# Slots of an expert kernel taken one block earlier: one at a part's second block, a slot inside the prologue, longer DMA runs and new order lists

## The chip, the cores and the metric

One core of a Trainium2 chip. The metric is the device time of one execution in microseconds (us), the median of several. Five engines work side by side: TensorE (PE, with its weight loads PEld), VectorE (DVE), ScalarE (ACT), GpSimd (POOL) and SyncE (SP, which here only issues DMAs).

## What is computed

Two layers, each a graph attention and a mixture of experts, on x of 128 graphs × 64 nodes × 256, that is N = 8192 tokens. Cut to what matters:

```python
def layer(x, adj, l):
    h = layernorm(x) @ W                       # 256 -> 256
    e = (h @ a1)[:, :, None] + (h @ a2)[:, None, :]    # 64 x 64 of a graph
    if l == 1: e = where(e > 0, e, 0.2 * e)
    x = x + elu(softmax(where(adj > 0, e, -9e15)) @ h)
    t = layernorm(x)
    # router: 8 experts, the best two of each token, softmax of the two
    # layer 0: x = x + t + sum over 2 of c * (gelu(t @ w1[e] + b1[e]) @ w2[e] + b2[e])   (256 -> 256 -> 256)
    # layer 1: x = x +     sum over 2 of c * (relu(t @ w1[e] + b1[e]) @ w2[e] + b2[e])   (256 -> 512 -> 256)
```

All in float32. Each layer has 8192 × 2 = 16384 pairs of token and expert.

## The kernel before

**Blocks.** A layer is 16 blocks of 512 tokens (4 tiles of 128). `attend` does the attention of a block, `route` the router. In `attend` a mask is made from adj on POOL (`cap_g`, L341), then statistics on DVE (their power −0.5 on POOL, L290), the normalisation on ACT (L299), transposes on PE (`pt_g`, L310), `pw_g` (L355), `pe_g` (L381), the exponentials on ACT, the scaling L399/L400 on DVE, the transposes `pp_g` (L404), `pT_bd` (L407 on DVE, L409 on ACT), `po_g` (L415), and the sum with x on DVE (L430 to L438). In `route` come statistics again, `tn_r` (L299, ACT), transposes `pt_r`, the router's product `plT_r` (L492), the transpose of the scores on DVE (`lg_r`, L503), the best two, and the counts of tokens by expert (`pn_r`, L553/L554).

**Lists.** Each expert has a list in HBM. For each tile t of a block, a cast of the positions to integers on DVE (`ix_r`, L582) is followed by two indirect DMAs issued by POOL (L587) which write the 128 rows of `tn_r` to the lists of their first and second expert. A row is 256 values and the token's number, expert and (layer 1) weights: 258 or 260 values, 1032 or 1040 B.

**Slots.** A slot is 256 rows of one expert. `plan` (L656 to L698, 20 small DVE instructions) works out on the chip which lists have 256 rows to give. With it `Slots.take` adds SB = 4 slots at each block from the third of a part on (b ≥ LAG = 2). Layer 0 has two parts (blocks 0 to 8 and 9 to 15), layer 1 one. At a part's end SR = 8 more are taken, and 7 that hold the rests of the lists, each 128 rows of one list, two lists to a slot. That makes 40 + 32 + 68 slots. A slot passes through:
- F: `fetch` reads its rows (`xg`, L780, issued by SP), W: its weights (`wc`, L834, L840, L845, SP; 4 buffers)
- x: transposes `px_s` (L900, PE) and their copy `xT` (L905, DVE)
- h: `ph_s` (L998, PE) with gelu or relu (L1008, ACT)
- y: `py_s` (L1034, PE) and `ys` (L1049, DVE; 4 buffers)
- p: layer 0, an indirect write to `res` (L1070, POOL); layer 1, after w (ACT, L1103), an indirect accumulating write into the output (L1080, POOL), each slot's behind the landing of the last one's.

Layer 1's blocks read `mid` (x with the attention and t) and the two rows of `res` of each token.

**Order.** The instructions of SP, PE, DVE and ACT stand in the order in which the program emits them. POOL's indirect DMAs are ordered by `pooled`. The emission is written out by hand: `PROLOGUE` until block 3's attention is done (aN and rN advance attention and routing of block N by a stage), then for each t from 3 to 31 one of two lists `STEPS` (layer 0, layer 1), in which a1 is attention of block t+1, a2 of t+2, r0, r1, r-1 routing, and x, h, y, p, w, W, F act on the oldest slot that has come so far; a mark ? or ! makes an entry hold only when more than four slots wait, or not. Then `ENDING[0]` and, until all slots are done, `ENDING[1]` in turns. In the prologue C0 and C1 make constants by an iota on POOL and a cast on DVE (`counted`), and F0 does the first fetch and the weights of four slots (`slots.ahead(4)`); no x, h, y or p stands in it.

In L598 the condition of taking is

```python
        if b - (CUT if b >= CUT and l == 0 else 0) >= LAG:
            slots.take(l, b, SB, plan(l, f"p{l}_{b}", SB))
```

and the layouts of `mid`, `res` and of a fetch are

```python
    mid_t = mid.rearrange("(b t p) d -> b p t d", t=TT, p=P)
    res_t = [r.rearrange("(b t p k) d -> b p t (k d)", t=TT, p=P, k=2) for r in res]
                out=xg[:, r, 0 : ROW[l]],
                in_=lists[l][bass.ds(u * rows, n), :].rearrange("(t p) d -> p t d", p=P),
```

so that a partition reads 1 KB rows of `mid`, 2 KB of `res` and two single rows of a list.

Of the kernel before, what the change touches and what calls it, by code (L numbers as in the profile page):

```python
# [16 lines left out]
P = 128  # L17
# [4 lines left out]
TT = 4  # L22
# [12 lines left out]
    "h2 h0 h1 a1 a1 p w h0 p p x0 a1 r-1 p h2 h3? r0 w a1 x1 R2 a1 a1 h1 a1 a1 L r-1 r0 "  # L35
    "r0 r0 x2 a1 h3 x0? x1? a1 r0 y0 r0 p a1 w a1 a1 a2~ r0 r-1 x2? p y1 R2 r-1 r-1 p r0 "
    "h2? a1 x1! p y2 a1 W W A2 r0 h0? p? a2~ r-1 h1? a1 R1 a2 y0 a1 w? y1 r0 h3 p F p R1 "
    "x0? x0 a1 y2 W W x1? r0 x2? x0! p? x1 a1 p a2 a2 x2! R1 a1 w? a1 h2 p a1 w h0 w h1 p "
    "p? y0? y1? x0 p p p a1 y2? p? p? h0 r1 y0 x2 p y1 p? h3 h2 a2 p R1 p x1 x2 r0 r1 p p "
    "r0 h3 F W h1 y2 w W W W E1 x0 p y0 p p a2 y1 x1 y2 Z w r1 r0 r0 r0 r1 W x2 W w W ",  # L40
    "a1 a1 a1 w L r-1 h0 r0 a1 h1 h2 p x0 r0 r0 a1 w x1 r-1 a1 h3 x2 r0 x0? p x0! x1? a1 "
    "R2 r0 a2~ x2? h0 p p R2 a1 a1 h1 a1 h3 r-1 r0 p r-1 h2 r0 p r-1 a1 a2~ a1 a1 r0 y0 "
    "r0 r-1 p a1 p w y1 y2 W W h0? h1? r0 x1! h2? h3? y0 p p? a1 a1 p? y1 a1 w? p p x2 y2 "
    "x0 x1 W W p A2 p a1 x2? a1 a1 x0? a1 W R1 w x2! h0 a2 a2 F h1 x1? p? y0? y1? a2 h2 "
    "a1 y2? W h3 p? x2 w w? x0 p h0 a2 p h1 h2 R1 x1 R1 w h3 p? p y0 r0 w p y1 a1 r1 r0 "
    "y2 W W r0 r1 y0 p p? p r1 p F x0 x1 a2 r0 r0 Z p p w p y1 y2 W E1 p x2 W R1 r0 r1 W ",
]
PROLOGUE = (
    "a0 a1 a0 a2 a0 a0 a0 a1 a1 a2 a0 a0 a2 G0 a1 a0 a0 a0 a1 a1 C0 a2 a0 a1 a0 C1 a0 a0 "
    "a0 a2 a0 a1 a2 a1 B0 a1 a0 a1 a1 B1 a2 a0 a1 a0 a1 a0 a0 a1 a2 a1 a0 a2 a1 a2 a0 a0 "  # L50
    "a2 a0 a3 a0 a0 L5 a1 a0 a3 a1 a1 a2 a2 a0 a0 r0 a2 a2 L4 a2 a1 r0 a1 a2 a1 r0 a1 a1 "
    "a2 r0 a2 r0 r0 a3 a3 a1 r0 a2 a2 a1 a2 a1 a1 a3 a4 P0 a2 r0 a2 a1 r0 r0 r0 r1 a2 r1 "
    "a3 a2 a2 a2 a4 a4 a3 r0 a3 r1 a2 a3 r1 a2 r1 a3 a4 a3 G1 a3 r2 r2 r1 r1 a3 r0 r0 a3 "
    "r2 r1 r0 r0 r1 a3 a3 r0 r2 r1 a3 r2 a3 r2 r0 r1 r2 r0 r0 r2 r0 a4 r0 r0 r2 a3 r1 a3 "
    "r0 r2 r1 r2 a3 r1 a3 a4 r0 r1 a3 r0 r2 r0 a3 r1 r1 r1 r1 r1 r2 r1 r2 a4 r1 r2 r1 r1 "
    "a3 a3 a3 a3 r2 r1 a3 r1 r2 r1 a3 r3 r2 r2 r2 r2 r2 r3 r2 r2 r2 r2 r2 F0 r3 r2 r3 "
)
ENDING = [
    "p h1 x1 x0 p p r p x2 w w h0 W h2 h3 ",
    "h3 w x1 r2 q y0 h0 h1 p y1 y2 W p W p p q x2 h2 x0 p W w p F r w ",  # L60
# [4 lines left out]
def adj_ffn_kernel(  # L65
# [44 lines left out]
    SR = SB * LAG  # L110
# [28 lines left out]
    mid_t = mid.rearrange("(b t p) d -> b p t d", t=TT, p=P)  # L139
    res_t = [r.rearrange("(b t p k) d -> b p t (k d)", t=TT, p=P, k=2) for r in res]  # L140
    sums_t = [mid_t, out_t]

    def part(b):

        return int(b >= CUT)

# [325 lines left out]
    def route(l, b, blk):  # L472
# [125 lines left out]
        if b - (CUT if b >= CUT and l == 0 else 0) >= LAG:  # L598
            slots.take(l, b, SB, plan(l, f"p{l}_{b}", SB))
# [169 lines left out]
    def fetch(sl, name):  # L769

        l, rows = sl["l"], P if sl["rest"] else SL
        xg = slot.tile([P, ST, ROW[1]], F32, tag="xg", name=f"xg_{name}", bufs=8)
        for s, r in sl["of"]:
# [7 lines left out]
                out=xg[:, r, 0 : ROW[l]],  # L781
                in_=lists[l][bass.ds(u * rows, n), :].rearrange("(t p) d -> p t d", p=P),
# [4 lines left out]
    class Slots:  # L787
# [105 lines left out]
        def x(self, k):  # L893
# [32 lines left out]
            if rest:  # L926
# [4 lines left out]
                for _, r in sl["of"]:  # L931
                    n = (r.stop - r.start) * P
                    for t in range(r.start, r.stop):
                        nc.vector.tensor_scalar(
                            le[:, t, 0:n], places[:, 0:n], free[:, t : t + 1], None, ALU.is_ge
                        )
# [397 lines left out]
```

## Time and profile before

| what | us |
|---|---|
| median of 8 runs | 1361.18 |
| lowest, highest | 1354.06, 1367.93 |
| the profiled execution | 1353.56 |
| its span | 1351.8 |
| PE, DVE, POOL, ACT busy | 1154.8, 898.8, 713.0, 653.6 |
| mean granted clock of PE | 0.939 of full |

The profile is of one execution, taken by the hardware. A row of a timeline has the start in us from the span's start, the duration in us (of the whole group, if several instructions are put together), engine, line, operation, the tiles out<-in, the count, and in brackets how long the engine had been idle before and what ended that. A row of waits has the engine and what it was about to do, what it waited for, and the total in us, the number of times and the longest. "remote" there is a wait whose end no semaphore event of the program explains; "issue" is time in which the engine waited for nothing that the profile shows. A row of windows has a stretch, its length, each engine's busy time in it (with the instructions that began in it), the clock granted to PE, the mean busy share of 16 DMA engines, and GB/s.

Full-clock prices of PE, from rows after 725 us: four transposes of 128×128 take 0.44 us, eight passes of 128×256 take 1.73 us. A slot of layer 0 is then 3.9 us (4 px, 8 ph, 8 py) and one of layer 1 7.4 us (4, 16, 16). In layer 0 a block takes about 35 us (`pn_r` of blocks 7, 8, 9: 242.6, 277.2, 312.2), in layer 1 38.4 us from block 6 on.

### The profile page before, as it was taken

The numbers are of one execution on the slowest core, as the hardware profiler recorded it, in microseconds if no ns is written. First come the engines' busy times: TensorE is split into PE (matmuls) and PEld (weight loads), VectorE is DVE, ScalarE is ACT, GpSimd is POOL, SyncE is SP. The second block draws the span as 40 slices with busy tenths as digits, with TensorE's granted clock in tenths as the row PEclk, the third lists the DMA queues.
The fourth block names the chain that finished last, engine by engine and source line by source line (L and its number), as shares of the span: only waits on it lengthen the run. The fifth ranks groups of instructions, "written<-read, shape, count | busy, mean of one in ns | idle before, by whom it ended". The sixth has DMA issues, their size and how long they took to land. (4 is left out here: it accounts for less than half of the span.)

```text
span 1351.8 us, 22479 instructions
## 1 busy us (share of the span) xinstructions
PE 1154.8 (85%) x6176; PEld 974.2 (72%) x6176; DVE 898.8 (66%) x3605; ACT 653.6 (48%) x1548; POOL 713.0 (53%) x698
## 2 busy tenths in 40 slices
PE   6658787877888888778789999999999999999990
PEld 5436665756776766667668888888788888889880
DVE  4767775867667778787677777777687766433330
ACT  5636554645555655446554445455454543333330
POOL 3273555553554655556554465655666656533333
PEclk9868888988898998989899999999999999999995
DMA  7637666666776687798789788888978778999843
GB/s 193 180 121 219 221 195 206 199 211 212 245 220 215 216 291 252 226 302 270 240 267 272 226 219 247 242 246 251 272 211 237 194 208 228 265 275 257 230 94 35
DMA packets 263854, 301.17 MB, mean 223 GB/s; under 512 B 39463, under 2 KB 225070, under 8 KB 263728
## 3 DMA queue, kind: packets, MB, share of 16 engines
q1 hardware_dynamic: 208288, 214.50, 51.8%
q0 software_dynamic: 38544, 68.46, 20.3%
q10 hardware_dynamic: 16896, 16.78, 3.6%
q8 instruction: 49, 0.80, 0.3%
q14 instruction: 77, 0.63, 0.1%
HBM read 202.80 MB, written 98.69 MB: 223 GB/s over the span
## 5 line engine op out<-in xcount | busy, mean ns | idle before, releaser
L998 PE MATMUL ph_s<-xT_s,wc_s 128*128 128x256 f32 (+1 forms) x1760 | 403.6, 378 | 23.4 <-DVE xT_s L905 15.2
L1034 PE MATMUL py_s<-wc_s,hT_s 128*128 128x256 f32 x1648 | 392.2, 387 | 8.7 <-ACT hT_s L1008 6.2
L998 PEld LDWEIGHTS ph_s<-xT_s,wc_s 128*128 128x128 f32 x1760 | 321.6, 197 | 69.9 <-DVE xT_s L905 17.9
L1034 PEld LDWEIGHTS py_s<-wc_s,hT_s 128*128 128x128 f32 x1648 | 310.4, 193 | 56.8 <-ACT hT_s L1008 10.2
L1080 POOL DMA_INDIRECT out_dram<-ys_s,to_s x135 | 213.4, 1581 | 231.1 <-DMA out_dram<-ys_s,to_s 104.4
L587 POOL DMA_INDIRECT lists<-tn_r,ix_r x256 | 248.9, 972 | 144.7 <-issue 83.9
L1070 POOL DMA_INDIRECT res<-ys_s,to_s x142 | 142.7, 1005 | 108.7 <-DVE ys_s L1049 63.3
L1008 ACT ACTIVATE hT_s<-ph_s,b_s 128x256 f32<-128x256 f32 (+1 forms) x284 | 114.0, 459 | 106.1 <-PE ph_s L998 48.7
L355 PE MATMUL pw_g<-gw,xt_g 128*128 128x258 f32 x512 | 127.6, 397 | 9.0 <-ACT wh_g L366 6.0
L1049 DVE TENSOR_TENSOR ys_s<-py_s,tb 128x512 f32<-128x512 f32 (+1 forms) x71 | 47.2, 665 | 128.7 <-PE py_s L1034 74.2
L905 DVE COPY xT_s<-px_s 128x512 f32<-128x512 f32 (+1 forms) x140 | 95.1, 679 | 47.0 <-PE px_s L900 25.8
L1103 ACT ACTIVATE ys_s<-ys_s,cf_s 128x256 f32<-128x256 f32 x135 | 61.5, 500 | 127.4 <-DVE ys_s L1049 116.7
L355 PEld LDWEIGHTS pw_g<-gw,xt_g 128*128 128x128 f32 x512 | 95.5, 196 | 27.8 <-ACT wh_g L366 6.7
L1008 ACT ACTIVATE hT_s<-ph_s,wc_s 128x256 f32<-128x256 f32 (+1 forms) x156 | 61.0, 451 | 63.8 <-issue 37.4
L366 ACT COPY wh_g<-pw_g 128x258 f32<-128x258 f32 x128 | 47.8, 377 | 86.5 <-PE pw_g L355 63.7
L299 ACT ACTIVATE xn_g<-xs,nb_g,rs_g 128x256 f32<-128x256 f32 x128 | 66.3, 589 | 46.9 <-DVE nb_g L293 34.8
L900 PE MATMUL px_s<-ident,xg_s 128*128 128x128 f32 x554 | 85.8, 278 | 0.0
L299 ACT ACTIVATE tn_r<-xb_g,nb_r,rs_r 128x256 f32<-128x256 f32 x128 | 66.2, 588 | 33.2 <-DVE nb_r L293 12.9
L290 POOL TENSOR_TENSOR rs_r<-ve_r,nhalf 128x4 f32<-128x4 f32 x32 | 33.7, 1052 | 88.6 <-DVE c_r L535 42.5
L415 PE MATMUL po_g<-wh_g,pT_bd 128*128 128x256 f32 x256 | 68.9, 415 | 12.9 <-ACT pT_bd L409 8.6
L404 PE MATMUL pp_g<-ident,ee_g 128*64 128x128 f32 x128 | 22.7, 308 | 65.5 <-DVE ee_g L400 60.6
L900 PEld LDWEIGHTS px_s<-ident,xg_s 128*128 128x128 f32 x554 | 70.7, 146 | 10.9 <-DVE ys_s L1049 0.3
(503 smaller groups left out, 1613.5 us busy)
## 6 DMA issues: line engine op xcount, KB each, us to landing
wc_s<-in_w_dram SPq DMA_DIRECT2D x142, 512.0 KB
wc_s<-in_w_dram SPq DMA_DIRECT2D x156, 256.0 KB
xg_s<-lists SPq DMA_DIRECT2D x64, 260.0 KB
xg_s<-lists SPq DMA_DIRECT2D x64, 258.0 KB
yb<-res SPq DMA_DIRECT2D x16, 1024.0 KB
wc_s<-bcat SPq DMA_DIRECT2D x78, 129.0 KB
xs<-in_x_dram SPq DMA_DIRECT2D x16, 512.0 KB
mid<-xb_g ACTq DMA_DIRECT2D x16, 512.0 KB
```

The costliest lines, as they stand in the source:

```text
L299: nc.scalar.activation(outs(t), xb[:, t, :], AF.Identity, bias=nb[:, t : t + 1], scale=rs[:, t : t + 1])
L355: nc.tensor.matmul(pw, lhsT=xt[:, k, t * P : (t + 1) * P], rhs=gw[l][:, k, :], start=(k == 0), stop=(k == KD - 1),)
L415: nc.tensor.matmul(po[h][:, j, :], lhsT=pT[:, 2 * h + j, :], rhs=wh[:, 2 * h + j, 0:D], start=True, stop=True,)
L587: ins = pooled(f"lists{l}", lambda: nc.gpsimd.indirect_dma_start(out=lists[l], out_offset=bass.IndirectOffsetOnAxis(ap=ix[:, k, t : t + 1] ...
L900: nc.tensor.transpose(px[:, c, t * P : (t + 1) * P], xg[:, t, c * P : (c + 1) * P], ident)
L905: nc.vector.tensor_copy(xT[:, :, 0 : st * P], px[:, :, 0 : st * P])
L998: nc.tensor.matmul(ph[:, j, r], lhsT=w[:, o : o + P], rhs=xT[:, c, r], start=(c == 0), stop=(c == KD - 1),)
L1008: nc.scalar.activation(hT[:, f + j, r], ph[:, j, r], AF.Gelu if l == 0 else AF.Relu, bias=(sl["b1"][i][:, f + j : f + j + 1] if l else w[: ...
L1034: nc.tensor.matmul(py[:, t, :], lhsT=hT[:, f, t * P : (t + 1) * P], rhs=w[:, O2[l] + f * D : O2[l] + (f + 1) * D], start=(f == 0), stop=(f ...
L1070: ins = pooled(group, lambda: nc.gpsimd.indirect_dma_start(out=res[sl["part"]], out_offset=self.row(sl, t), in_=sl["ys"][:, t, :], in_offs ...
L1080: ins = pooled("sums", lambda: nc.gpsimd.indirect_dma_start(out=out, out_offset=self.row(sl, t), in_=sl["ys"][:, t, :], in_offset=None, co ...
L1103: nc.scalar.activation(sl["ys"][:, t, :], sl["ys"][:, t, :], AF.Identity, scale=sl["cf"][:, t : t + 1])
```

## The change

1. One slot is taken at the second block of a part (b = LAG − 1, three times in all, each with a plan of its own on DVE), four at each later block as before, and at a part's end SR = 7 and the rests. The number of slots stays.
2. The prologue fetches once more, earlier (F0 stands twice), and ends with x0 x1 x2 h0 h1: the first slot's transposes, copy, ph and activation stand among the first blocks, ahead of block 4's `pt_g` on PE.
3. Runs are longer: a partition of `mid` and `res` holds the four tiles of its tokens side by side (4 and 8 KB), and one of `xg` two neighbouring rows of a list (2064 B in layer 0). Token numbers, places and their constants follow; `place` and `places` are made in two sizes each (two more pairs of iota and cast).
4. All lists are new. PE's, DVE's and ACT's orders within a block change in places; in layer 0 the last of the four casts L582 of a block now stands behind L405 and ys on DVE, and one slot is always further along. In layer 1 the casts that precede the block's L503 go from eight to four.

The diff, with the lists cut:

```diff
-    SR = SB * LAG
+    SR = SB * LAG - 1
...
-    mid_t = mid.rearrange("(b t p) d -> b p t d", t=TT, p=P)
-    res_t = [r.rearrange("(b t p k) d -> b p t (k d)", t=TT, p=P, k=2) for r in res]
+    mid_t = mid.rearrange("(b p t) d -> b p t d", t=TT, p=P)
+    res_t = [r.rearrange("(b p t k) d -> b p t (k d)", t=TT, p=P, k=2) for r in res]
...
+    def nth(l, b):
+
+        return b - (CUT if b >= CUT and l == 0 else 0)
...
-        if b - (CUT if b >= CUT and l == 0 else 0) >= LAG:
-            slots.take(l, b, SB, plan(l, f"p{l}_{b}", SB))
+        n = SB if nth(l, b) >= LAG else int(nth(l, b) == LAG - 1)
+        if n:
+            slots.take(l, b, n, plan(l, f"p{l}_{b}", n))
...
-        xg = slot.tile([P, ST, ROW[1]], F32, tag="xg", name=f"xg_{name}", bufs=8)
+        xg = slot.tile([P, ST * ROW[1]], F32, tag="xg", name=f"xg_{name}", bufs=8)
+        xg = xg[:, 0 : ST * ROW[l]].rearrange("p (t d) -> p t d", t=ST)
...
-                out=xg[:, r, 0 : ROW[l]],
-                in_=lists[l][bass.ds(u * rows, n), :].rearrange("(t p) d -> p t d", p=P),
+                out=xg[:, r, :],
+                in_=lists[l][bass.ds(u * rows, n), :].rearrange("(p t) d -> p t d", p=P),
...
-                sl["place"] = place[:, 0:st] if whole else place[:, 0:1].to_broadcast([P, ST])
+                sl["place"] = place[st - 1] if whole else place[0].to_broadcast([P, ST])
...
-            token2 = counted("token2", [P, NT], [[2 * P, NT]], 0, 2)
+            token2 = counted("token2", [P, NT], [[2 * TB, NB], [2, TT]], 0, 2 * TT)
...
-            place = counted("place", [P, ST], [[P, ST]], 0, 1)
+            place = [counted(f"place{n}", [P, n], [[1, n]], 0, n) for n in range(1, ST + 1)]
...
-            places = counted("places", [P, SL], [[1, SL]], 0, 0)
+            places = [counted(f"places{n}", [P, n * P], [[1, n], [n, P]], 0, 0) for n in range(1, ST + 1)]
...
+        elif w in "xhy":
+            slots.phase(w, i)
+        elif w == "p":
+            slots.put()
...
-            slots.ahead(4)
+            slots.ahead(min(4, len(slots.need)))
```

The end of PROLOGUE and the second ENDING, before and after:

```diff
-    "a3 a3 a3 a3 r2 r1 a3 r1 r2 r1 a3 r3 r2 r2 r2 r2 r2 r3 r2 r2 r2 r2 r2 F0 r3 r2 r3 "
+    "a3 a3 a3 r2 r1 a3 r1 r2 r1 r1 F0 a3 r2 r3 r2 r2 r2 r2 r3 r2 r2 r2 r2 r2 F0 r3 r2 r3 "
+    "x0 x1 x2 h0 h1 "
...
-    "h3 w x1 r2 q y0 h0 h1 p y1 y2 W p W p p q x2 h2 x0 p W w p F r w ",
+    "x1 W r2 y0 h0 p q h1 h3 w y1 y2 h2 p p x0 W p W w F x2 w p r q p ",
```

## The prediction

> **What bounds the kernel now.** I read the busy shares first, then a table of windows, then the waits, then two stretches of the timeline. The page's first lines:
>
> ```profile
> PE 1154.8 (85%) x6176; PEld 974.2 (72%) x6176; DVE 898.8 (66%) x3605; ACT 653.6 (48%) x1548; POOL 713.0 (53%) x698
> ...
> PEclk9868888988898998989899999999999999999995
> ```
>
> PE is busy for 1154.8 of 1351.8 us, so 197.0 us are left. The windows (length, then PE, PEld, DVE, ACT, POOL, the granted clock, the DMA share) tell where:
>
> ```profile
> 75.00:100.00 25.00, 11.39 (x48) 7.79 (x46) 14.73 (x71) 6.74 (x16) 18.27 (x19) 0.65 0.32 112
> ...
> 200.00:300.00 100.00, 77.75 (x421) 63.81 (x420) 67.43 (x265) 54.06 (x120) 56.50 (x57) 0.90 0.66 211
> ...
> 645.00:700.00 55.00, 42.34 (x251) 34.85 (x250) 38.51 (x146) 29.27 (x62) 29.16 (x30) 0.94 0.74 230
> 700.00:725.00 25.00, 22.86 (x106) 19.76 (x107) 21.56 (x86) 10.14 (x28) 11.56 (x11) 0.93 0.99 325
> 725.00:767.00 42.00, 41.34 (x224) 35.91 (x223) 26.54 (x110) 19.76 (x52) 22.88 (x19) 1.00 0.78 213
> ...
> 1000.00:1300.00 300.00, 297.95 (x1614) 262.05 (x1613) 162.20 (x679) 121.53 (x309) 152.15 (x115) 1.00 0.86 235
> 1325.00:1351.00 26.00, 0.00 (x0) 0.00 (x0) 0.00 (x0) 0.00 (x0) 9.33 (x7) 0.50 0.31 36
> ```
>
> There are three regimes. Up to about 725 us PE idles a fifth of the time and a chain through DVE, POOL and ACT sets the pace of a block. From 725 to 1300 us PE itself is the bound, at full clock. The last 26 us hold no PE work, only POOL's accumulating writes. The number of slots is the same after the change, 140, and so is PE's work. A gain can therefore come from PE work put into idle time before 725 us, from shorter waits there, or from the tail. The waits that carry this are one of PE's, the one of DVE behind it, and POOL's at the tail:
>
> ```profile
> PE pp_g L404 <- DVE ee_g L400: 60.6, 16, 8.4
> ...
> DVE lg_r L503 <- remote: 29.5, 5, 7.7
> ...
> POOL out_dram L1080 <- DMA out_dram<-ys_s,to_s: 104.4, 26, 7.0
> ```
>
> Block 9's stretch shows how the first two hang together:
>
> ```profile
> 292.38 0.96 POOL L587 DMA_INDIRECT lists<-tn_r,ix_r  x1 [0.30 <-issue]
> 293.65 0.96 POOL L587 DMA_INDIRECT lists<-tn_r,ix_r  x1 [0.30 <-issue]
> 294.92 0.96 POOL L587 DMA_INDIRECT lists<-tn_r,ix_r  x1 [0.30 <-issue]
> 295.95 1.07 POOL L341 TENSOR_SCALAR cap_g<-adj 128x256 f32<-128x256 int32 x1
> 297.76 0.32 DVE L503 STREAM_TRANSPOSE lg_r<-plT_r 128x128 f32<-128x128 f32 x1 [7.70 <-remote]
> ...
> 299.89 1.03 PE L404 MATMUL pp_g<-ident,ee_g 128*64 128x128 f32 x4 [8.42 <-DVE ee_g L400]
> ```
>
> DVE stands still for 7.70 us in front of the transpose L503 while POOL issues list writes (one each 1.27 us) and then makes the mask L341. The transpose starts 0.74 us after the mask ends. L400 stands behind it on DVE, and PE's L404 waits for L400. The same happens in block 7 (7.70 us, start 229.22, the mask last too). In blocks 6, 10 and 11 (4.08, 6.14, 3.86) the list writes are last.
>
> **Part 1: slot 0 among the first blocks.** Before, the prologue looks like this:
>
> ```profile
> 79.85 1.97 PE L310 MATMUL pt_g<-ident,xn_g 128*128 128x128 f32 x8 [0.91 <-DVE xb_g L430]
> 91.05 1.95 PE L310 MATMUL pt_r<-ident,tn_r 128*128 128x128 f32 x4 [9.23 <-ACT tn_r L299]
> 92.79 5.11 PE L355 MATMUL pw_g<-gw,xt_g 128*128 128x258 f32 x16
> ...
> 100.48 3.11 SPq L780 DMA_DIRECT2D xg_s<-lists  x4
> ...
> 104.51 1.06 PE L900 MATMUL px_s<-ident,xg_s 128*128 128x128 f32 x4
> ```
>
> In the new order slot 0's px and ph stand on PE ahead of block 4's pt_g, and an extra plan stands on DVE. A plan is 20 instructions, from 86.23 to 90.15, so 3.9 us; the one of block 1 comes ahead of block 3's statistics. Those, now ready at 83.8, become ready near 88 to 90. The fetch of slot 0 needs that plan and blocks 0 and 1 in the lists (last write 86.53 + 0.96 = 87.5): issued near 89. From issue to px took 4.03 us (100.48 to 104.51), so px0 starts near 93. Then its copy (0.68) and ph (3.78 us for 8 matmuls at the clock of this stretch, as L415 at 107.03) give ph's end near 99; 8 transposes of pt_g (1.97) end at 101 at the worst, 99 if the copy overlaps less badly. So pw_g starts near 100 where it started at 92.79: +7.2. PE has then been working, and the block after it had pw_g in 3.65 us (122.03) rather than 5.11: −1.5. Of slot 0, py (1.99) now stands ahead of pp_g, where PE idled for 2.84: hidden. Sum **+6**. Bounds: +3, if the statistics are not late (the 9.23 us wait of pt_r absorbs slot 0); +20, if the fetch is issued only behind block 2's lists, as the first one is now (98.71 + 1.77; then px at 104.5 to 107).
>
> **Part 2: the last cast of a block's positions is moved behind L405.** In layer 0 three of the four casts L582, not four, precede the transpose on DVE, so POOL's last pair of list writes (2 × 1.27) and, in odd blocks, the mask (1.07) come behind it. In blocks 7 and 9 the burst was t1, t2, t3, mask without a gap: minus 3.61, less the half microsecond by which list writes release later than the mask (1.2 to 1.65 after their end, not 0.74): −3.1 each, **−6.2**. In blocks 6, 8, 10 and 11 the last pair already stood behind a result write that waited for ys: nothing. Bounds: 0, if the burst only moves or another wait (esm on ACT, py ahead) takes its place; −15.4, if both waits of 7.70 go whole. What is late next is L400's other input, ACT's exponentials, early by at least the wait.
>
> [...]
>
> **Part 3: one slot more is done before layer 1's block 4.** Counted in the order of both kernels, the new one is one slot ahead from the prologue on and level with the old one at layer 1's block 4 (75 py and 84 ph in both). So PE has a slot less to do between blocks 1 and 4 of layer 1 (645 to 767 us), where it idles for 55.00 − 42.34 + 2.14 + 0.66 = 15.5 us only. A slot at full clock is 3.9 us in layer 0 and 7.4 in layer 1 (0.44 + 3.46 + 3.46). I take **−5**, the nearer of a layer-0 slot with its clock loss; bounds 0 (the stretch is bound by DVE, 21.56 of 25, and not by PE) and −7.4.
>
> **Part 4: three more plans on DVE.** One is in part 1. The other two (blocks 10 and 1 of layers 0 and 1) are 3.9 us each. DVE has 30 of 100 us free in layer 0, so part of it falls into waits such as those for POOL: **+1** together, bounds 0 and +7.8.
>
> **Part 5: longer runs.** The list fetch goes from 1032 B to 2064 B a run, mid from 1 to 4 KB, res from 2 to 8 KB. PE waits for no fetch (px has 0.0 us idle before it), so it can only help where the DMA share is near one: 700 to 725 us (0.99, PE short by 2.14) and the accumulating writes from 1200 us on, whose next issue waits for the last to land (104.4 us in all). Queue q1 moves 208288 packets of 1030 B in 51.8% of 16 engines, 53.8 ns each; whether a packet twice as long takes twice that no row shows. Bounds 0 and −8; I take **−2.5**. Two more iota and cast pairs in the prologue are about 0.5 us of DVE, hidden in its 5 to 14 idle us of each early window. [...]
>
> **Part 6: the tail.** It runs at POOL's pace: five last slots 6.4 us apart (1317.15, 1323.54, 1330.01, 1336.37, 1342.68), some 20 us behind PE. The new ending has one normal slot more ahead of the pairs: **0**, ±2.
>
> **The sum.** 6 − 6.2 − 5 + 1 − 2.5 + 0 = −6.7 us on the profiled execution's 1353.56 (span 1351.8 and 1.8 around it): 1346.9. That execution is 0.6% under the median of the eight runs, 1361.18, which is the scale of the forecast: **1354.5 us**, −0.5%.
>
> **Rivals.**
> 1. **Slot 0 stops block 4** (slower). PE executes in list order, so until slot 0's rows have landed nothing of block 4 starts. If px0 starts at 104 to 107 and not 93, part 1 is +17 to +20 and the sum +4 to +7; with part 3 at 0 as well, since layer 1's start is bound by DVE, +9 to +12: 1370. It decides from a px0 later than about 100. For: the 9.23 us wait shows that this stretch has no slack, and the clock there is the lowest (0.65). Against: the plan of block 1 is on DVE 10 us before that of block 2.
> 2. **Nothing gained in layer 0** (no change). The burst moves, and L503 waits for it a few us later, or pp_g waits for a py that now stands ahead of it. Part 2 is 0 and −0.5 is left: 1360.7. For: two more plans on a DVE that these blocks already wait for.
> 3. **The DMA relief reaches the tail** (faster). The accumulating writes keep up with PE from 1200 us on, and the 20 us lag shrinks by two slots' 6.4: −6.7 − 12.8: 1342. For: their spacing there is 7.5 to 10 us beside 6.4 in the empty tail. Against: bytes are the same, and ys has only four buffers, so the lag was already held.
>
> **The numbers.** Forecast (−2 to −12) 0.48; rival 1 0.24; rival 2 0.15; rival 3 0.13. The range leaves out the outer half of rivals 1 and 3 and runs from 1341 to 1370. Half a per cent, 6.8 us, is about what a measurement tells here from no change. Beyond it on the fast side lie rival 3 and about 0.3 of the forecast; within it the rest of the forecast, rival 2 and a little of rival 1: 0.43, 0.35, 0.22.
>
> **What would show it.** Part 1: pw_g of block 4 near 100 and pn_r of block 3 near 122 (115.98 before). Part 2: L503's wait under 5 us in blocks 7 and 9, and the PE line above down from 60.6 by 6. Part 3: PE busy for more than 0.8 between blocks 1 and 4 of layer 1, and layer 1's later blocks again 38.4 us apart. Part 5: less time per byte on q1. I am wrong if px0 comes after 100, if L503 waits as long for fewer writes, or if the saturated stretch changes its length.

## The result, and the profile after

| | before | after |
|---|---|---|
| median, us | 1360.19 (1348.33 to 1373.28, 56 runs) | 1377.71 (1366.91 to 1390.27, 20 runs) |
| span of the profiled execution | 1351.8 | 1374.4 |
| mean granted clock of PE | 0.939 | 0.927 |

The ratio is 1.0136 (95% interval 1.0114 to 1.0158): the change made the kernel slower by 17.5 us, the difference of the medians. (The ratio leaves out executions over 1.5% above the fastest of their kernel, so it is not quite the quotient of the medians.) The forecast was 1354.5 with a range up to 1370, so it was wrong in sign and in range. The two profiled executions stand 22.6 us apart: before's (1353.56 us) was one of its quicker ones.

In the new kernel the lines of this part are 5 to 7 higher (L503 is L508, L404 is L409, L385 is L390, L290 is L295, L587 is L592, L998 is L1005). First the page's busy shares and clock:

```profile
PE 1165.7 (85%) x6168; PEld 979.1 (71%) x6168; DVE 909.9 (66%) x3659; ACT 654.4 (48%) x1550; POOL 718.3 (52%) x700
...
PEclk9858898898999999899998999999999999999995
```

Then the same windows (length, PE, PEld, DVE, ACT, POOL, clock, DMA share, GB/s):

```profile
75.00:100.00 25.00, 9.84 (x32) 7.32 (x32) 17.30 (x94) 8.59 (x17) 16.17 (x17) 0.51 0.42 142
...
645.00:700.00 55.00, 43.61 (x233) 36.23 (x232) 42.63 (x168) 31.80 (x67) 25.99 (x26) 0.88 0.71 230
700.00:725.00 25.00, 18.76 (x111) 14.60 (x109) 17.68 (x66) 11.13 (x24) 16.61 (x16) 0.98 0.90 310
725.00:767.00 42.00, 40.11 (x200) 33.91 (x201) 31.37 (x126) 20.97 (x54) 15.59 (x12) 0.89 0.69 202
```

PE's work is the same but takes 10.9 us more, at a lower clock. PE has less done in the first window (9.84 for 11.39) and, against the plan, less from 700 to 725 us (18.76 for 22.86). Next the waits, one row of PE, two of DVE and POOL's at the accumulating writes:

```profile
PE pp_g L409 <- DVE ee_g L405: 31.3, 12, 5.7
...
DVE lg_r L508 <- remote: 27.7, 6, 5.1
...
DVE ee_g L390 <- remote: 20.6, 4, 5.7
...
POOL out_dram L1087 <- DMA out_dram<-ys_s,to_s: 126.6, 30, 7.5
```

PE's wait for L405 fell from 60.6 to 31.3, and yet the kernel is slower. L508 lost 1.8 us of its 29.5. The wait of the same kind at `ee_g` is new in this size: 0.7 before, now 20.6. POOL waits longer at the accumulating writes (104.4 before); by itself that is no loss, for the version with the lowest ratio of all has 122.2 there (e5). To see where the time went I cut each trace at `pn_r` of some blocks ("l1 4" is block 4 of layer 1):

| stretch, us | before | after | difference |
|---|---|---|---|
| start to block 2 | 78.25 | 79.11 | +0.9 |
| block 2 to 5 | 92.3 | 105.1 | +12.8 |
| block 5 to 15 | 365.4 | 359.0 | −6.4 |
| block 15 to l1 4 | 191.7 | 204.0 | +12.2 |
| l1 4 to l1 15, the "saturated stretch" | 425.5 | 424.2 | −1.3 |
| l1 15 to the end | 198.5 | 203.0 | +4.4 |

**Blocks 2 to 5.** The prologue in PE's timeline:

```profile
92.81 1.12 PE L907 MATMUL px_s<-ident,xg_s 128*128 128x128 f32 x4 [12.63 <-DMA xg_s<-lists]
95.21 3.78 PE L1005 MATMUL ph_s<-xT_s,wc_s 128*128 128x256 f32 x8 [1.29 <-DVE xT_s L912]
98.78 1.30 PE L315 MATMUL pt_g<-ident,xn_g 128*128 128x128 f32 x8
```

px0 at 92.81, ph's end at 98.99, block 4's pw_g at 100.43 and block 3's `pn_r` at 123.07: forecast were 93, 99, 100 and 122. But block 4 comes another 5.5 us later and block 5 another 1.0 (+7.1, +12.6, +13.6).

**Block 15 to l1 4.** Layer 1's block 2 in the timeline of POOL, DVE and PE:

```profile
641.20 0.96 POOL L592 DMA_INDIRECT lists<-tn_r,ix_r  x1 [0.30 <-issue]
...
644.02 0.42 DVE L390 TENSOR_TENSOR ee_g<-pe_g,cap_g 128x256 f32<-128x256 f32 x1 [5.68 <-remote]
...
648.43 1.03 PE L409 MATMUL pp_g<-ident,ee_g 128*64 128x128 f32 x4 [2.65 <-DVE ee_g L405]
```

The first row is the last of eight list writes that POOL issues back to back from 632.14 on. In the kernel before, the same eight came as two, two and four, with a result write between and this gap ahead of the last four:

```profile
623.33 1.04 POOL L587 DMA_INDIRECT lists<-tn_r,ix_r  x1 [1.88 <-issue]
```

L390 now stands behind all four casts and waits until about the time at which the writes have landed (their last packet ends at 643.25), and the attention of the block stands behind it. The same happens at 565, 685 and 725 us. Around the last one PE runs empty and then loses its clock, in windows:

```profile
720.00:724.00 4.00, 1.38 (x5) 0.57 (x4) 0.00 (x0) 0.00 (x0) 2.63 (x3) 0.99 1.06 398
724.00:734.00 10.00, 7.11 (x18) 5.14 (x19) 5.49 (x23) 4.64 (x14) 2.06 (x2) 0.50 0.62 192
```

DVE and ACT stand still for the whole first 4 us, and then PE gets half its clock for 10 us.

### The profile page after: what moved, and what is told of

Read it like the earlier page. It is cut to its first block, busy times and chain, and to the rows that moved or that the text cites. A ratio compares the mean times of both kernels' runs of the same rounds, so it can differ in the third digit from the quotient of the medians.

```text
span 1374.4 us, 22495 instructions
## 1 busy us (share of the span) xinstructions
PE 1165.7 (85%) x6168; PEld 979.1 (71%) x6168; DVE 909.9 (66%) x3659; ACT 654.4 (48%) x1550; POOL 718.3 (52%) x700
## 3 DMA queue, kind: packets, MB, share of 16 engines
q1 hardware_dynamic: 179616, 214.50, 50.4%
q0 software_dynamic: 38544, 68.46, 19.5%
## 4 chain that ended last, share of the span: by engine, by line
PE 56%; DVE 19%; DMA 6%; issue 5%; ACT 5%; another core or an unknown queue 5%; POOL 2%; SPq 0%; DVEq 0%; POOLq 0%; ACTq 0%
PE ph_s L1005 20%; PE py_s L1041 17%; PE pw_g L360 6%; DMA out_dram<-ys_s,to_s 4%; PE px_s L907 3%; PE po_g L420 2%; PE pt_r L315 2%; PE pt_g L315 2%; DVE st_r L289 2%; DVE ys_s L1056 2%; DVE xb_g L438 1%; DVE xT_s L912 1%; PE pp_g L409 1%; ACT hT_s L1015 1%
## 5 line engine op out<-in xcount | busy, mean ns | idle before, releaser
L1005 PE MATMUL ph_s<-xT_s,wc_s 128*128 128x256 f32 (+1 forms) x1760 | 411.3, 382 | 40.0 <-DVE xT_s L912 29.0
L1041 PE MATMUL py_s<-wc_s,hT_s 128*128 128x256 f32 x1648 | 402.8, 390 | 23.2 <-ACT hT_s L1015 17.4
L1005 PEld LDWEIGHTS ph_s<-xT_s,wc_s 128*128 128x128 f32 x1760 | 328.5, 199 | 94.9 <-DVE xT_s L912 35.6
L1087 POOL DMA_INDIRECT out_dram<-ys_s,to_s x135 | 218.3, 1617 | 241.8 <-DMA out_dram<-ys_s,to_s 126.6
L592 POOL DMA_INDIRECT lists<-tn_r,ix_r x256 | 249.8, 976 | 146.1 <-issue 86.5
L360 PE MATMUL pw_g<-gw,xt_g 128*128 128x258 f32 x512 | 124.4, 389 | 6.8 <-DVE du_p_15r L658 1.8
L912 DVE COPY xT_s<-px_s 128x512 f32<-128x512 f32 (+1 forms) x140 | 95.2, 680 | 44.5 <-PE px_s L907 27.7
L907 PE MATMUL px_s<-ident,xg_s 128*128 128x128 f32 x554 | 87.6, 282 | 12.6 <-DMA xg_s<-lists 12.6
L907 PEld LDWEIGHTS px_s<-ident,xg_s 128*128 128x128 f32 x554 | 71.3, 150 | 21.7 <-DMA xg_s<-lists 12.8
L409 PE MATMUL pp_g<-ident,ee_g 128*64 128x128 f32 x128 | 24.4, 326 | 61.6 <-DVE ee_g L405 31.3
L295 POOL TENSOR_TENSOR rs_r<-ve_r,nhalf 128x4 f32<-128x4 f32 x32 | 33.8, 1055 | 74.8 <-DVE c_r L540 32.2
```

Source lines behind the costliest of these rows:

```text
L360: nc.tensor.matmul(pw, lhsT=xt[:, k, t * P : (t + 1) * P], rhs=gw[l][:, k, :], start=(k == 0), stop=(k == KD - 1),)
L592: ins = pooled(f"lists{l}", lambda: nc.gpsimd.indirect_dma_start(out=lists[l], out_offset=bass.IndirectOffsetOnAxis(ap=ix[:, k, t : t + 1] ...
L907: nc.tensor.transpose(px[:, c, t * P : (t + 1) * P], xg[:, t, c * P : (c + 1) * P], ident)
L912: nc.vector.tensor_copy(xT[:, :, 0 : st * P], px[:, :, 0 : st * P])
L1005: nc.tensor.matmul(ph[:, j, r], lhsT=w[:, o : o + P], rhs=xT[:, c, r], start=(c == 0), stop=(c == KD - 1),)
L1041: nc.tensor.matmul(py[:, t, :], lhsT=hT[:, f, t * P : (t + 1) * P], rhs=w[:, O2[l] + f * D : O2[l] + (f + 1) * D], start=(f == 0), stop=(f ...
```

## The experiments

My theory after the result: the earlier slot costs the start some 14 us (the plan, the slot, the new prologue); layer 1's list costs some 9 us through L390; the longer runs give nothing. The main rival: the runs themselves slow the saturated stretch. Each "ratio" is against the kernel before on the same chip (95% interval). Stretches are block 2 to 5, 5 to 15, 15 to l1 4, l1 4 to l1 15, l1 15 to the end.

| run | ratio | stretches of its profile, us |
|---|---|---|
| e1 runs only | 1.0063 (1.0026 to 1.0101) | 91.7, 360.1, 199.0, 435.9, 200.2 |
| e2 old lists | 1.0116 (1.0051 to 1.0182) | 98.8, 363.1, 191.3, 434.2, 199.6 |
| e3 no slot in prologue | 1.0116 (1.0037 to 1.0195) | 105.3, 356.4, 202.8, 424.7, 203.2 |
| e4 old STEPS | 1.0114 (1.0030 to 1.0198) | 105.4, 364.8, 193.9, 431.9, 202.5 |
| e5 before, write moved | 0.9943 (0.9912 to 0.9974) | 94.2, 354.9, 199.1, 418.3, 200.3 |
| e6 the same on e1 | 0.9975 (0.9943 to 1.0007) | 94.0, 361.5, 195.7, 420.3, 201.0 |
| e7 without the runs | 1.0177 (1.0103 to 1.0251) | 109.2, 361.2, 198.7, 430.6, 203.2 |
| e8 old PROLOGUE | one execution, 1364.68 us | 101.9, 357.3, 200.7, 427.9, 196.1 |
| e9 last cast behind | 1.0147 (1.0103 to 1.0191) | 112.3, 358.3, 191.4, 426.8, 203.8 |
| e10 old layer 1 list, write moved | 1.0038 (0.9999 to 1.0076) | 109.1, 359.5, 186.5, 416.1, 204.0 |
| e11 old lists, write moved | 0.9993 (0.9960 to 1.0026) | 106.6, 361.0, 191.3, 416.1, 201.1 |
| e12 e11, mark ? from five | 1.0090 (1.0054 to 1.0126) | 99.8, 367.9, 197.9, 416.0, 201.5 |
| *chips on which before takes 1291 us* | | |
| e13 five at the third block | 0.9950 (0.9918 to 0.9981) | 95.2, 317.1, 173.0, 415.9, 205.3 |
| e14 the same without the runs | 0.9976 (0.9951 to 1.0002) | 97.8, 317.1, 171.9, 415.9, 208.8 |
| e15 only layer 0's new list | 0.9961 (0.9931 to 0.9991) | 97.3, 317.5, 170.3, 416.1, 203.2 |
| e16 the changed kernel | 1.0105 (1.0074 to 1.0136) | 106.6, 315.6, 170.4, 424.1, 202.4 |
| e17 as e15 | 0.9968 (0.9945 to 0.9992) | 96.8, 315.0, 170.6, 415.9, 202.6 |
| e18 as e13 | 0.9947 (0.9921 to 0.9974) | 96.8, 317.2, 169.7, 415.9, 201.5 |

The kernel before took 1351 to 1364 us on the chips of the upper rows. Stretches of the two groups are not compared. Within the upper group the first stretch scatters by some 8 us between executions of like kernels (e2, e8, e11, e12: 98.8 to 106.6) and the second by 10 (before, e1, e5, e6: 354.9 to 365.4), so of a profile there only what recurs counts.

### e1: the longer runs alone

Part 3 of the diff on the kernel before:

```diff
-    mid_t = mid.rearrange("(b t p) d -> b p t d", t=TT, p=P)
+    mid_t = mid.rearrange("(b p t) d -> b p t d", t=TT, p=P)
...
-                in_=lists[l][bass.ds(u * rows, n), :].rearrange("(t p) d -> p t d", p=P),
+                in_=lists[l][bass.ds(u * rows, n), :].rearrange("(p t) d -> p t d", p=P),
```

> The kernel before with the longer runs alone (part 5). Theory that the runs are worth nothing, since q1 needed 50.4% of 16 engines over 1374.4 us after and 51.8% over 1351.8 us before, for the same 214.5 MB (1.1% less time per byte): ratio to before 0.998 to 1.003. Rival, my part 5 as forecast: 0.995 to 0.998, with the accumulating writes waiting less than 104.4 us. Rival, the runs cost something (the lists' landing is later): over 1.004, and then they are part of the 17 us.

No gain: at 1.0063 the last rival of the three came, the runs cost something. In after's trace 2064 B packets of layer 0 take 115.4 ns in the mean, in before's 1032 B ones 55.1, so nothing is saved per byte. The loss is in the saturated stretch, where four blocks take 42 to 45 us instead of 38.44. One of them, in the timeline:

```profile
1049.97 1.60 POOL L1081 DMA_INDIRECT out_dram<-ys_s,to_s  x1 [3.55 <-issue]
1051.04 1.62 POOL L290 TENSOR_TENSOR rs_g<-ve_g,nhalf 128x4 f32<-128x4 f32 x1
1052.69 0.16 DVE L293 SCALAR_TENSOR_TENSOR nb_g<-mv_g,rs_g 128x4 f32<-128x4 f32 x1 [6.59 <-POOL rs_g L290]
...
1060.18 0.33 PE L310 MATMUL pt_r<-ident,tn_r 128*128 128x128 f32 x1 [2.67 <-ACT tn_r L299]
```

On POOL an accumulating write stands ahead of the small `rs_g`, and POOL idles 3.55 us in front of it. (By the program each such write waits for the landing of the one before; this row names no releaser.) DVE waits 6.59 us for `rs_g`, all that stands behind it is late, and PE waits 2.67 us for `tn_r`. The windows around that:

```profile
1057.00:1061.00 4.00, 1.17 (x5) 0.39 (x3) 2.96 (x19) 2.27 (x5) 2.52 (x2) 1.00 0.66 229
1061.00:1064.40 3.40, 3.22 (x9) 2.48 (x9) 2.32 (x7) 2.72 (x7) 2.67 (x3) 0.50 0.64 70
```

The granted clock is 0.50 for the 3.4 us after the stall. The kernel before has the same waits in a milder form (up to 2.15 us; blocks of 39.3 to 42.0), and there the clock holds. Its whole saturated stretch, in a window:

```profile
727.73:1153.27 425.54, 419.33 (x2274) 363.21 (x2273) 311.19 (x1262) 203.38 (x526) 253.30 (x202) 1.00 0.85 234
```

So layer 1's middle was not at PE's bound, as I had read it: 425.5 us where eleven blocks without a wait take 10 × 38.44 + 31.56 = 416.0. Of the 9.5 us PE idles 6.2 (425.54 − 419.33); the other 3.3 are longer matmuls at a clock of 1.00.

### e2, e3, e4: which part of the lists

e2 is the changed kernel with all lists of before, e4 with its STEPS only (the STEPS of before), e3 without the slot in the prologue:

```diff
-    "x0 x1 x2 h0 h1 "
```

> The changed kernel with PROLOGUE, STEPS and ENDING of the kernel before; the taking of slots and the longer runs stay. Theory that the new order costs the time: ratio to before 0.997 to 1.004, block 3's pn_r at about 116 to 117. Rival, the taking of one slot at a part's second block costs it, through three more plans of 3.9 us on VectorE: 1.006 to 1.012, with the loss at blocks 3, 10 and layer 1's block 1.

> The changed kernel without x0 x1 x2 h0 h1 at the prologue's end; all else stays, the first slot then runs in the first step. Theory that slot 0's place costs 7 us in block 3 and about 3 of the 5.5 us in block 4, and that nothing later gives it back: ratio to before 1.005 to 1.009. Rival, the slot must then run in a layer-0 block at the chain's pace and costs there what it saved: 1.012 to 1.016. Second rival, later phases fall out of step with the new lists: over 1.016.

> The changed kernel with the STEPS of before; its new PROLOGUE (slot 0 in it) and ENDING stay. Theory that the loss of 5 us in each of block 4, layer 1's block 0 and layer 1's block 2 comes from the new order in the steps: ratio to before 1.004 to 1.008, with the prologue's 7 us still there. Rival, these losses come from having one slot more under way, whatever the order: 1.011 to 1.016.

Within their intervals (four executions each) all three are as slow as the whole change, so none of these pieces is seen to carry it alone. In e2 and e4 the rival's range came and not the theory's; e3 fell between the two. In e2 the early plan alone delays block 3's `pt_r` by 3.74 us (94.79 for 91.05). In e3 nothing is gained, and so the place of the slot is not separated from the rest of the new prologue: slot 0's px then stands at the head of the first step, ahead of `pt_r`, and waits 9.15 us there for its rows. e4 has the old stretch from block 15 on (193.9) and the long saturated one (431.9).

### e5, e6: the write behind rs_g

One mark of layer 1's old list is moved, on the kernel before (e5) and on e1 (e6). Nine blocks change on POOL, nothing else:

```diff
-    "x0 x1 W W p A2 p a1 x2? a1 a1 x0? a1 W R1 w x2! h0 a2 a2 F h1 x1? p? y0? y1? a2 h2 "
+    "x0 x1 W W p A2 p a1 x2? a1 a1 x0? a1 W R1 w x2! h0 a2 a2 F h1 x1? y0? y1? a2 p? h2 "
```

> The kernel before with one entry of its second list moved: p? from ahead of the a2 that emits rs_g (L290) to behind it, so that in layer 1's blocks 7 to 15 POOL computes rs_g ahead of an accumulating write, not behind it. PE's and ACT's orders do not change. Theory that PE loses its time in layer 1's saturated blocks because rs_g stands behind a write that waits for the landing of the one before: from block 6 of layer 1 on, blocks of 38.44 us and no wait of PE for tn_r over 0.5 us; 3 to 8 us less than before, ratio 0.994 to 0.998. Rival, the write that is now later makes the next one later, and rs_r behind it: 0.999 to 1.004, with PE's waits for tn_r as before.

> The same move in the kernel with the longer runs alone, whose ratio to before was 1.0063 and whose layer-1 blocks were 42 to 45 us long every second time. Theory that the runs cost time only through the place of rs_g on POOL: ratio 0.994 to 1.000, the same as the move in the kernel before within 0.003. Rival, the runs cost it elsewhere, in landings that all wait for: 1.004 or more, about 0.006 above the move in the kernel before.

e5 beats the kernel before, 0.9943. PE's waits between 770 and 1150 us, in before and then in e5:

```profile
PE pt_r L310 <- ACT tn_r L299: 5.5, 14, 2.2
```

```profile
PE pt_r L310 <- ACT tn_r L299: 0.8, 5, 0.2
```

The stretch takes 418.3 us in place of 425.5, and seven of its ten full blocks take 38.44. The theory's range came in both. With the write moved, the runs of e6 cost nothing that can be told (the intervals of e5 and e6 overlap, though 0.3% between them isn't excluded), and the stretch that they lengthened to 435.9 us in e1 takes 420.3. So what the runs did there went through this wait.

### e7, e8: the rest without the runs, and without the new prologue

e7 is the changed kernel with the old layouts (e1's diff backwards), e8 with the old PROLOGUE. All of its lines change, here the last:

```diff
...
-    "a3 a3 a3 r2 r1 a3 r1 r2 r1 r1 F0 a3 r2 r3 r2 r2 r2 r2 r3 r2 r2 r2 r2 r2 F0 r3 r2 r3 "
-    "x0 x1 x2 h0 h1 "
+    "a3 a3 a3 a3 r2 r1 a3 r1 r2 r1 a3 r3 r2 r2 r2 r2 r2 r3 r2 r2 r2 r2 r2 F0 r3 r2 r3 "
```

> The changed kernel with the old layouts of mid, res and fetches; slots, prologue and lists stay. Theory that the runs' cost belongs to the old list of layer 1, which the new list does not share (its PE stalls in the saturated blocks are 0.5 to 0.7 us before ph, none before pt_r): ratio 1.011 to 1.016, as the changed kernel. Rival, the runs cost 0.6% in either order: 1.005 to 1.009.

> The changed kernel with the PROLOGUE of before; the taking of slots, the new STEPS and the new ENDING stay. One look, for the start times of the blocks. Theory that slot 0's place ahead of block 4 costs the 7 us of block 3 beyond the 3.7 us of the plan: pn_r of block 3 at 117 to 120 (123.07 in the changed kernel, 117.34 with all old lists). Rival, it is the new first list that makes the first slot's px wait: 123 to 125, as without x0 to h1 in the prologue (124.33).

e7, at 1.0177, is no better than the change: the runs don't carry the loss, and the rival falls. e8 is one execution only. Block 3's `pn_r` comes at 116.35 (123.07 in the changed kernel), so its rival, the new first list, falls. Three of L390's four waits are there with 5.6 us each, so they don't come from the prologue.

### e9: the last cast behind L390

```diff
-    "R2 r0 r-1 x2? h0 a2~ p R2 a1 h3 a1 h1 a1 p h2 r0 p r-1 a2~ r0 r-1 a1 a1 r0 y0 r-1 p "
+    "R2 r0 r-1 x2? h0 a2~ p R2 a1 h3 a1 h1 a1 p h2 r0 p r-1 a2~ r0 a1 a1 r0 y0 r-1 r-1 p "
```

> The changed kernel with one entry of its second list moved: the r-1 that emits the last cast of a block's positions goes from ahead of L390 to behind L508, so that in layer 1 two of the eight list writes are no longer in the run that L390 waits out (4.25, 5.68, 5.65 and 5.00 us in the profile of the changed kernel, none in the kernel before). Theory that this new wait is where the gain forecast for layer 1's start went: L390's waits down by 2.5 us each (two writes of 1.27), layer 1's blocks 0 to 4 shorter by 6 to 10 us together, ratio to before 1.005 to 1.011. Rival, the wait only moves to L508 or to the next operation that needs PE: waits of the same sum there, 1.011 to 1.016.

L390's "remote" waits went from 20.6 to 3.1 us, and the stretch from block 15 to l1 4 from 204.0 to 191.4. But part of the wait only changed its name. At the same instruction e9 has

```profile
DVE ee_g L390 <- PE py_s L1041: 6.0, 3, 2.4
```

so 9.1 us are left. And the total did not follow: 1.0147, in the rival's range. In the profiled execution the start took 7 us more than after's, which is as large as the scatter there, and the edit does not touch the start; where the other executions lost it, I can't show. So that L390's waits cost the change its time in total is not shown, and this one stays open.

### e10: the old list in layer 1

The changed kernel with the old STEPS[1], its write moved as in e5; layer 0's list, prologue, ending, taking and runs are the new ones.

> The changed kernel with the second list of the kernel before, and in it the write moved behind rs_g as before. Prologue, first list, ending, slots and runs are the changed kernel's. Theory: no L390 waits, layer 1's blocks 0 to 5 take some 192 to 196 us from layer 0's last pn_r (204 in the changed kernel, 191.7 before), the saturated blocks 416 to 419; what is left is the loss of the first five blocks, some 13 us, less the slot done ahead: ratio 0.999 to 1.006. Rival, that the loss of the first five blocks is all there is and layer 1's list matters little: 1.009 to 1.014.

1.0038, as the theory had it: 0.98% (± 0.44) less than the change, some 13 us. That is the new list of layer 1 against the old one with the write moved. The move alone was worth 0.57% on the kernel before (e5), so, if the two add up, some 0.4% is left for the new list against the old one as it was, which the intervals don't tell from nothing. The profiles differ in both of layer 1's stretches: 204.0 and 186.5, 424.2 and 416.1.

### e11, e12: the old lists with the write moved, and the mark "?"

e11 is e2 with e5's diff. e12 asks whether the five waiting slots do harm through the mark "?", which is true from five on:

```diff
-        more = slots.nf - slots.ny > SB or len(slots.all) - slots.ny > SB
+        more = slots.nf - slots.ny > SB + 1 or len(slots.all) - slots.ny > SB + 1
```

> All lists of the kernel before with the write moved behind rs_g, the new taking of slots and the longer runs. Theory that the taking by itself is about even (13.7 us late at block 9, given back to 3.2 us at layer 1's block 4 in the kernel without the move), once rs_g is out of the way: saturated blocks 416 to 419, ratio 0.994 to 1.001, within 0.004 of the move with the runs alone (0.9975). Rival, the taking costs through its plans: 1.003 to 1.009.

> The same with the conditional entries of the lists decided at more than five slots instead of four, since one more slot is now under way in every block. Theory that the early loss of the taking (blocks 3 to 9) comes from entries marked ? that now hold a block sooner and put a ys ahead of the next block's statistics: pn_r of block 9 at 309 to 314 (321.5 with the threshold of four), ratio 0.988 to 0.995. Rival, the loss is the plan and the slot themselves: 318 or more at block 9, and the same ratio as with the threshold of four.

e11 is level with before (0.9993), where e5, without the early slot and the runs, is at 0.9943: together they cost 0.50% (± 0.45). Against e6, which has the runs too, the early slot alone is 0.18% (± 0.46), not told from nothing. e12 is slower (1.0090), and `pn_r` of block 9 comes at 327.3 where 309 to 314 were expected: that theory fell.

### e13, e14, e15: other cuts

e13 is e11 with no slot at layer 0's second block and five at its third, e14 the same with the old layouts, e15 the changed kernel with the old PROLOGUE and e5's STEPS[1], so with the new list in layer 0 alone.

```diff
+        if l == 0 and b < LAG + 1:
+            n = (SB + 1) * int(b == LAG)
```

> All lists of the kernel before with the write behind rs_g, longer runs, and the taking changed in layer 0's first part alone: none at the second block, five at the third; the later parts take one at their second block. Theory that the loss of the first blocks (pn_r of block 2 to that of block 5: 93 us with the old taking, 99 to 107 with the new one under the old lists) is the plan of 3.9 us and the slot put where PE's clock is lowest: 93 to 97 us in that stretch, and with layer 1's start still 4 us shorter a ratio of 0.990 to 0.996. Rival, the loss comes from five slots under way in place of four: 99 or more in that stretch, ratio 0.997 to 1.003 as with the slot at the second block (0.9993).

> The same without the longer runs. Theory that the runs are worth nothing once rs_g stands ahead of the write: within 0.004 of the one with the runs. Rival, they cost 0.3% as the pair with and without them suggested (0.9975 and 0.9943): 0.003 to 0.006 less than with them.

> The changed kernel with the prologue of before and the second list of before with the write behind rs_g: of the lists only the first and the ending are new. Theory that the new prologue costs 6 us beyond the taking (pn_r of block 2 to that of block 5: 105 to 112 us with it, 99 to 107 without): 100 to 104 us there, ratio 0.996 to 1.001 against 1.0038 with the new prologue. Rival, the prologue's place of slot 0 is even: ratio 1.002 to 1.006.

They fell on a chip where before itself takes 1291 us. e13 and e15 are faster than before, 0.9950 and 0.9961. And in none of the three traces does DVE have a "remote" wait, which in before's came to 29.5 us at L503 alone. Blocks 5 to 8 of layer 0 take 27 to 31 us there where before's took 34 to 38. No profile of before was taken on these chips.

### e16, e17, e18: the chip or the kernel

> The changed kernel itself, beside the two best versions so far, on whatever chip this falls on. Open: in the runs of five_at_third_block, five_without_runs and new_first_list VectorE had no wait at all for TensorE's late counter behind the list writes (29.5 us at L503 in the profile of before, 27.7 + 20.6 us in that of the changed kernel), and before itself took 1291 us there against 1351 to 1364 elsewhere. Theory A, the chip sets that wait: on a chip where before takes some 1350 to 1364 us the wait is there, and the ratio is again 1.010 to 1.016; on a chip where before takes some 1290 us the wait is gone, the layer 1 list loses its 20.6 us of waits, and the ratio is 0.995 to 1.004. Theory B, the wait came from the order of those three kernels and the chip is only quicker in general: on a quick chip the changed kernel still shows 15 us or more of waits at L390 and a ratio over 1.008.

> The kernel of new_first_list: the changed kernel with the prologue of before and with the layer 1 list of before whose accumulating write stands behind rs_g. Theory A (the chip sets the waits): on a chip with the waits, summed from the stretches of the earlier runs: +8.7 (new taking, old prologue), -1.9 (new layer 0 list), -4.2 (a slot less at layer 1's start), -11 (the moved write), +2 (the end) = about -6, ratio 0.993 to 1.000, with 20 to 30 us of waits at L508; on a chip without, 0.996 again and no such wait. Theory B (the order of this kernel removed the wait): no wait at L508 on any chip, and a ratio far under 0.98 on a chip where before has its waits.

> The kernel of five_at_third_block: the lists of before with the moved write, longer runs, and no slot at layer 0's second block but five at its third. Theory A: on a chip with the waits +2 (start), +3.7 (new taking with the old steps), -2, -11, +2 = about -5, ratio 0.994 to 1.001, with 20 to 30 us of waits at L508; on a chip without, 0.995 again. Theory B: no waits on any chip, and a ratio under 0.98 where before has them.

They fell on another such chip (before 1290.62), where e17 and e18 repeat e15 and e13. The changed kernel has no "remote" wait there either, so the chip (or something that went with it) sets it, not the order. Of one kernel, the profiles of after and e16 differ in the stretches ahead of the saturated one, 359.0 and 315.6, 204.0 and 170.4, and not in it, 424.2 and 424.1. In that theory A is right; its ratio is not. I expected 0.995 to 1.004, and 1.0105 (1302.47 us) came. Against e17 (1283.58 us) the profiles show 9.8 us more from block 2 to 5, nothing more from there to l1 4, and 8.1 us more in the saturated stretch. With the last goes this row of DVE's waits of e16:

```profile
DVE nb_g L298 <- POOL rs_g L295: 25.4, 11, 3.8
```

In e17 it is

```profile
DVE nb_g L297 <- POOL rs_g L294: 6.5, 6, 1.7
```

One block of e16 in the timeline:

```profile
826.18 1.60 POOL L1087 DMA_INDIRECT out_dram<-ys_s,to_s  x1 [3.58 <-ACT q_r L534]
827.25 1.61 POOL L295 TENSOR_TENSOR rs_g<-ve_g,nhalf 128x4 f32<-128x4 f32 x1
828.89 0.16 DVE L298 SCALAR_TENSOR_TENSOR nb_g<-mv_g,rs_g 128x4 f32<-128x4 f32 x1 [3.02 <-POOL rs_g L295]
...
834.94 1.99 PE L1005 MATMUL ph_s<-xT_s,wc_s 128*128 128x256 f32 x8 [1.10 <-DVE xT_s L912]
```

The new list still has the write ahead of `rs_g`. There PE waits up to 1.6 us for a slot's copy `xT` (1.1 in this block), and nine of the ten full blocks take 38.5 to 40.4 us instead of 38.44. The saturated stretches of e16 and e17, in windows:

```profile
670.88:1094.96 424.08, 419.14 (x2273) 363.26 (x2272) 312.72 (x1270) 204.32 (x526) 260.22 (x204) 1.00 0.86 237
```

```profile
662.49:1078.43 415.94, 415.94 (x2274) 363.16 (x2272) 313.26 (x1269) 204.16 (x526) 256.51 (x204) 1.00 0.87 242
```

Of the 8.1 us PE idles 4.9, nearly all of it for `xT`, and 3.2 are longer matmuls at a clock of 1.00. That the write's place is the cause is argued from the rows: the move of e5 was not tried in the new list.

## Why the prediction was wrong

**The reading of the bound.** Wrong in one regime. I took 1000 to 1300 us at clock 1.00 for the whole of 725 to 1300 us. The clock is indeed 1.00 there, but PE's waits of up to 2.2 us, and the longer matmuls beside them, cost 9.5 us (425.5 against 416.0). They show in the blocks' times: five of ten take 39.3 to 42.0 us, the last of them 41.96, so "38.4 us from block 6 on", as I had described the kernel before, was wrong. I had not listed them one by one. The largest gain found in the kernel before was there and not in what the change touched: e5, −0.57%.

**Part 1 (+6).** This step failed in both groups of chips. In the one profile of after, block 3 comes +7.1 late, right to about a microsecond, with px0, ph and pw_g where the forecast had them; that the size fits is in part luck. The failed step is that the sum ended at that block. By means of the profiles on the slower chips the stretch from block 2 to 5 takes 93.1 us with the old taking (before, e1, e5, e6), 101.8 with the new taking and the old prologue (e2, e8, e11, e12), and 107.7 with the new prologue (after, e3, e4, e7, e9, e10): +8.7 and +5.9, so +14.6 where +6 was forecast. By block, block 3 is +8.9, block 4, which the sum left at nothing, +5.3, and block 5 +0.5. On the chip of e16 the new prologue costs +9.8 against e17. The taking itself is not seen on the quicker chips: e15 and e17 take 97.3 and 96.8 us with a slot at the second block, e13, e14 and e18 95.2, 97.8 and 96.8 without. That blocks 3 to 5 are a chain in which plan and slot stand with their whole time is my reading; what in the new prologue costs the time is not separated (e3).

**Part 2 (−6.2).** In blocks 7 and 9 the wait fell from 7.70 to 5.06 and 5.05, near the −3.1 each. Block 8 lost 3.75 (0.41 to 4.16), so the waits at this line fell by 1.8 in all. From block 5 to 15 the mean is 358.6 us with the new list (after, e3, e7 to e10) against 364.2 at the same taking (e2, e4, e11, e12), −5.6, which is near the forecast in size but mostly not by its mechanism, and within a scatter of 10; on the quicker chips, with no such wait, it is about −1 (means 316.0 and 317.1). What ends the 7.70 us shows in before's trace: DVE starts 0.02 us after a count from PE arrives, and in blocks 7 and 9 that count comes 0.6 us after the last packet of the list writes (0.0 to 0.8 us over all "remote" waits of before and after at this line and at L390). On the quicker chips there is no wait for it at all (no "remote" row in e13 to e18).

**Part 3 (−5).** This step failed on the slower chips. The gain of a slot isn't refuted: from block 15 to l1 4 the mean is 196.4 us with the old taking (before, e1, e5, e6) and 192.2 with the new one under the old list (e2, e4, e11), −4.2; but single profiles lie between 191.7 and 199.1 with the old taking, so it isn't shown either. Under the new list it is 201.6 (after, e3, e7, e8), +9.4. I had written in the description of the change that four casts instead of eight precede L503 in layer 1, and priced only layer 0's casts. That another wait takes the place of the one removed was the bound of 0 in part 2 and rival 2; it came true in layer 1, at L390, with 20.6 us of waits in after's profile. What that is worth in total is open: e9, with less than half of those waits, is as slow as the change, and on the chip of e16 this term is zero (170.4 against 170.6) and the change still costs 1.05%.

My sign for part 3, PE busy for more than 0.8 between blocks 1 and 4 of layer 1, could not tell: from 645 to 767 us it is 0.87 before and 0.84 after.

**The saturated stretch (0).** It kept its length in the profile of after (425.5 and 424.2) but not its make-up: the new list takes away the waits for `tn_r` and the longer matmuls beside them (9.5 us) and puts waits for `xT`, again with longer matmuls (8.3 us), in their place. Without either wait the same work takes 416 us (e10 to e18, e16 aside).

**Parts 4 to 6.** In e2 a plan delays block 3's `pt_r` by 3.74 us, near the 3.9 forecast; the other two plans were not separated. The runs (−2.5) show no gain: e7 lies beside after, e14 beside e13, e6 beside e5, and under the old list of layer 1 they cost 0.63% (e1). The packets fit that: 55.1 ns for 1032 B and 115.4 for 2064 B, in the mean. The end is some 2 us longer on the slower chips (means 202.2 and 200.3, single profiles 196.1 to 204.0) and not longer on the others.

**The sum.** With the means of the slower chips, the new order and taking against the old: +14.6 (block 2 to 5), −1.9 (5 to 15, part 2 less what the taking costs there), +5.2 (to l1 4), −4 (the saturated stretch, 426.9 against 430.7 in before and e1), +2 (the end) = +16, against +17.5 measured. With single profiles scattering by 5 to 10 us in a stretch, a sum that fits so well is partly luck. Rival 1 (a late px0) did not happen; the loss had its size by other terms. Nor did any of my three signs of being wrong come in after's profile (px0 at 92.81, L503's waits in blocks 7 and 9 shorter, the saturated stretch as long as before), so they watched the wrong places.

## What to carry to other kernels

Price a reordering at every place where it moves an instruction past a queue, in each list, and follow a delay until a stretch with slack takes it up, not to the first block where the arithmetic closes. List the blocks' times one by one before calling a stretch saturated: a 2 us stall that recurs shows there at once. Its remedy (a small operation that others wait for goes ahead of a slow, waiting DMA issue on the same queue, in e1's row 1.60 us behind 3.55 us of idling) was worth 0.57%, about what this whole change was forecast to bring. If a gain rests on a wait that the program doesn't explain, measure it on more than one chip. And when a run removes a wait, look at what the same instruction then waits for, and at the total: in e9 6.0 of 20.6 us stayed at the same instruction under another name, and the total did not move.

## What the hardware showed

- DVE's "remote" waits behind bursts of POOL's list writes are there on the three chips of e1 to e12 and absent on the two of e13 to e18, where the same kernel before takes 1291 instead of 1351 to 1364 us. The packets take the same time on both kinds, by the queues' shares: the 38544 of q0 111 ns each in after and 114 in e13 and e15, the 179616 of q1 62 ns in all three. Why PE's count arrives late on some chips stays open.
- PE's clock, 1.00 in before from 703 to 1324 us, was 0.50 in e1 from 1061.00 to 1064.40, and in after for 10.2 us from 723.95 on. At two more places in e1 eight passes of ph took 3.12 and 2.94 us (898.13 and 978.42), against 1.89 at 908.82. In the 4.00 us ahead of the two falls PE was busy for 1.17 us in e1 (from 1057.00) and 1.38 in after (from 720.00). But 0.99 us in e1 (from 813.35) and 1.85 in before (from 969.50) were followed by no fall: ph took 1.89 us again in e1, and before's clock stayed at 1.00. So PE's busy time alone doesn't settle it, and what does stays open.
